# A Mamba-2 block with a ternary FFN on one core: a new order for the last two sequences' steps

## The chip, the cores and the metric

The kernel runs on one core of a Trainium2 chip. The core has five engines that run side by side, each working through its own queue of instructions in order: TensorE (PE in the profile, its weight loads PEld), VectorE (DVE), ScalarE (ACT), GpSimd (POOL) and SyncE (SP, which here only starts DMA transfers). They wait for each other through semaphores. The metric is the device time of one execution in microseconds (us); lower is better. Three runs of the kernel before took 1191.03, 1191.05 and 1191.07 us, with a median of 1191.05 us.

## The reference

The input is x with 16 sequences of 512 tokens and 256 features, in float32. Cut to what matters, each sequence goes through this:

```python
x1 = layernorm(x)
z, xBC, dt = split(x1 @ in_proj_w.T)                 # 512, 768 and 8 columns
xs, B, C = split(silu(causal_conv4(xBC) + conv_b))   # 512, 128, 128
dt = softplus(dt + dt_bias); dA = exp(-dt * exp(A_log))
for t in range(512):                                 # 8 heads of 64
    S = dA[t] * S + (xs[t] * dt[t]) outer B[t]
    y[t] = S @ C[t] + D * xs[t]
g = y * silu(z)
att = x1 + (g * rsqrt(mean(g * g) + 1e-5) * norm_w) @ out_proj_w.T
x2 = x + layernorm(att)
x3 = layernorm(x2)
ffn = gelu(x3 @ ternary(W1).T + b1) @ ternary(W2).T + b2
out = x2 + layernorm(ffn)
```

## The kernel before

The sequences are numbered 0 to 15. One of them has 512 tokens, cut into NC = 4 chunks c of P = 128. The scan over time is done chunk by chunk: inside a chunk as a masked product, and from chunk to chunk through a state of 128x512 values. The work on a sequence b is split into stages, written as generators that issue a few instructions, yield an amount of work, and go on when they are asked again:

- `stage_a*` and `stage_b0`, `stage_d`, `stage_b1` make the projections, the convolution, the step sizes, the decay factors (`dec`), the masked decay matrices (`mts`, one for each chunk) and the tile `ct`, which `stage_d` fills by a DMA of 1.5 MB.
- `stage_e(b)` (L525) multiplies `ct` by C, one POOL instruction on 128x1024 values for each of the chunks 1, 2 and 3.
- `stage_b2(b)` (L555) is the scan. `prepare(c)` transposes the chunk (PE `px`), scales it (DVE `xdt`), makes the products of B and C (PE `pg`), copies B (DVE `bT`), scales the chunk for the state (POOL `xend`) and multiplies into `mts` (DVE, L608). Then, for each chunk, PE computes the chunk's own state (`pst`, L625); POOL decays the old state and DVE adds (`state`, L630 and L633); PE computes the outputs `py` (L641, and from chunk 1 on also L648, which reads the old state and `ct`); DVE adds the skip term (`y`, L654); POOL multiplies by the gate (`zs`, L658). `squares(c, y)` squares on ACT (L569) and adds twice on POOL (L570, L571); `root` sums over features on PE (`pss`, L577) and takes the inverse root on POOL (L582).
- `stage_c1(b)` (L672) begins with the squares of the last chunk, then runs out_proj for the four chunks (PE `po`, L707) with the layer norm statistics of `att` on DVE. After the fourth chunk `second_stream` makes x2 (DVE, L693) and its statistics; `normal` makes x3 (ACT, L285); then x3 is transposed (PE `pt_f`, L733) and split into three bfloat16 parts `x3p` (ACT L736, DVE L737 `rests`, ACT L740, POOL L741).
- `stage_c2(b)` (L745) is the FFN: eight blocks `ph` (PE, L753), each with a gelu (ACT, L759) into `hT`, and then four chunks of `pf` (PE, L787), each followed by DVE (`o`, L793), layer norm, the addition of x2 on POOL (L779) and the DMA of the result. The first two blocks are opened with the first two bfloat16 parts and closed with the third.
- `ending()` (L825) issues the last half of the previous sequence's result: two DVE instructions (L293), one on POOL (L779), one DMA.

The order within each engine's queue is the order in which the program issues the instructions; `manual_schedule` fixes it for PE, ACT, POOL and DVE. What interleaves the stages is `interleave` (L812). A stream is a tuple of stage, its whole work w, a start lo and an end hi. The stream whose position is lowest goes next, and on a tie the one listed first:

```python
at = [lo + (hi - lo) * done / w for _, w, lo, hi, done in live]
i = at.index(min(at))
```

Most of the kernel is a loop in which each sequence's projections stand beside the out_proj of the sequence before, and its scan beside that sequence's FFN. At the end there is nothing left to project. After `stage_a6(15)`, one call of `interleave` (L905) holds the last half of the result of sequence 13, the out_proj and FFN of sequence 14, and `stage_e`, the scan and the out_proj of sequence 15. The call after it runs the FFN of sequence 15 alone.

Tiles live in rings of a fixed number of buffers. PSUM has three: `ps_a` (4 buffers: `px`, `pst`, `py`, and `po` of sequence 15), `ps_tr` (2: `pg`, `pss`, `pt_f`) and `ps_c` (2: `po` of sequence 14, `ph`, `pf`). A new tile waits until the one that had its buffer has been read. In SBUF, `ct`, `att` (shared by `att` and x3), `hT`, `o` (shared with `rests` of sequence 14), `x2` of sequences 0 to 14, `x3p` and `sq` have a single buffer; `y`, `xdt`, `bT`, `xend` and `state` have two.

Of the kernel before, what the change touches and what calls it, by code (L numbers as in the profile page):

```python
# [57 lines left out]
def mamba_ffn_kernel(  # L58
# [18 lines left out]
    NB = x.shape[0]  # L77
# [16 lines left out]
    def load_x(b):  # L94
        xt = io.tile([P, NC, DM], F32, tag="xin", name=f"xin_{b}")
        nc.sync.dma_start(xt, x[b].rearrange("(c p) d -> p c d", p=P))
        xin[b] = xt
# [427 lines left out]
    def stage_e(b):  # L525

        s = seqs[b]
        xbc, ct = s["xbc"], s["ct"]
        for c in range(1, NC):
            nc.gpsimd.tensor_tensor(  # L530
                ct[:, c - 1], ct[:, c - 1],
                xbc[:, 5, c * P : (c + 1) * P].unsqueeze(1).to_broadcast([P, NH, P]), ALU.mult,
            )
            yield 0.7 if c == 1 else 0.15
# [20 lines left out]
    def stage_b2(b):  # L555
        s = seqs[b]
        dt, xbc, zs, dec, mts = s["dt"], s["xbc"], s["zs"], s["dec"], s["mts"]
        ct = s.pop("ct")

        def over_d(t):  # L560
            return t.unsqueeze(2).to_broadcast([P, NH, HD])
# [110 lines left out]
    def stage_c1(b):  # L672
        s = seqs[b]
        g, x1 = s["zs"], s["x1"]
        att = one.tile([P, NC, DM], F32, tag="att", name=f"att_{b}")
        s.pop("squares")()
        rms = s["rms"]

        last = b == NB - 1
        if last:  # L680
            x2 = io.tile([P, NC, DM], F32, tag="xin", name=f"x2_{b}")
            rests = io.tile([P, NC, DM], F32, tag="xin", name=f"rests_{b}")
            rests = rests.rearrange("p c d -> p (c d)").rearrange("p (k t) -> p k t", k=2)
        else:
            x2 = one.tile([P, NC, DM], F32, tag="x2", name=f"x2_{b}")
        x3 = one.tile([P, NC, DM], F32, tag="att", name=f"x3_{b}")
        norm_c, norm_f = Norm(att, f"c{b}"), Norm(x2, f"f{b}")

        def second_stream(lo, hi):


            for c in range(lo, hi):
                nc.vector.scalar_tensor_tensor(  # L693
                    x2[:, c, :], att[:, c, :], norm_c.rs[:, c : c + 1], xin[b][:, c, :],
                    ALU.mult, ALU.add,
                )
                norm_f.stats(c)
            norm_f.offset(lo, hi)

        yield 0.05  # L700
        for c in range(NC):
            if last:
                po = ps_a.tile([P, L], F32, tag="a", name=f"po_{b}_{c}")
            else:
                po = ps_c.tile([P, L], F32, tag="c", name=f"po_{b}_{c}")
            for k in range(NJ):
                nc.tensor.matmul(  # L707
                    po[:, 0:DM], g[:, k, c * P : (c + 1) * P], wo_sb[:, k, :],
                    start=(k == 0), stop=(k == NJ - 1),
                )  # L710
            if c == 2:
                s.pop("root")()
            nc.vector.scalar_tensor_tensor(  # L713
                att[:, c, :], po[:, 0:DM], rms[:, c : c + 1], x1[:, c, :], ALU.mult, ALU.add
            )
            norm_c.stats(c)
            if c % 2 == 1:
                norm_c.shift(c - 1, c + 1)
            if c == 3:
                second_stream(0, 2)  # L720
                second_stream(2, 4)
                if b + 3 < NB:
                    load_x(b + 3)
            yield (0.1, 0.07, 0.01, 0.33)[c]
        norm_f.normal(x3, 0, 1, 2, 3)
        yield 0.22
        if not last:
            rests = one.tile([P, 2, L], F32, tag="o", name=f"rests_{b}")
        x3p = one.tile([P, 3, 2, L], BF16, tag="x3p", name=f"x3p_{b}")
        for k in range(2):  # L730
            pt = ps_tr.tile([P, 512], F32, tag="tr", name=f"pt_f{b}_{k}")
            for c in range(NC):
                nc.tensor.transpose(  # L733
                    pt[:, c * P : (c + 1) * P], x3[:, c, k * P : (k + 1) * P], ident
                )
            nc.scalar.copy(x3p[:, 0, k, :], pt)  # L736
            nc.vector.tensor_sub(rests[:, k, :], pt, x3p[:, 0, k, :])  # L737
        yield 0.12
        for k in range(2):
            nc.scalar.copy(x3p[:, 1, k, :], rests[:, k, :])  # L740
            nc.gpsimd.tensor_sub(x3p[:, 2, k, :], rests[:, k, :], x3p[:, 1, k, :])  # L741
        s.update(x2=x2, x3p=x3p, shift=norm_c.off)
# [69 lines left out]
    def interleave(*streams):  # L812


        live = [[g, w, lo, hi, 0.0] for g, w, lo, hi in streams]
        while live:
            at = [lo + (hi - lo) * done / w for _, w, lo, hi, done in live]
            i = at.index(min(at))
            step = next(live[i][0], None)
            if step is None:  # L820
                live.pop(i)
            else:
                live[i][4] += step

    def ending():  # L825
        while endings:
            endings.pop()()
        yield 0.1
# [4 lines left out]
    E_WORK = 1.0  # L833
    A0_WORK, T0_WORK, A_WORK, A2_WORK, B1_WORK, B2_WORK = 1.0, 0.9, 18.1, 1.0, 0.5, 14.9
    C1_WORK, C2_WORK = 1.0, 24.2
# [10 lines left out]
    def run(stage):  # L846
        for _ in stage:
            pass

    with tc.manual_schedule(engines=ordered):  # L850
        nc.vector.memset(rhs_e[:, 0], 0.0)
        nc.vector.memset(lhs_e, 0.0)
        interleave(
            (
                chain(stage_a0(0), stage_t0(0), stage_a(0, EVEN)),
                A0_WORK + T0_WORK + A_WORK, 0.0, 1.0,
            ),
            (exponent_constants(), 9.0, 0.15, 0.9),
            (stage_a0(1), A0_WORK, 0.4, 0.9),
        )  # L860
        run(stage_t0(1))
        run(stage_a1(0))
        interleave(
            (stage_a2(0), A2_WORK, 0.0, 0.6),
            (scales(), 6.0, 0.35, 0.9),
            (stage_a(1, EVEN), A_WORK, 0.0, 1.0),
        )
        run(stage_a1(1))
        run(stage_b0(0))
        run(stage_d(0))  # L870
        for i in range(NB - 1):
            if i > 0:
                interleave(
                    (ending(), 0.1, 0.0, 0.01),
                    *([(ternary(2), 4.0, 0.1, 0.7)] if i == 1 else []),
                    *([(stage_a6(i), 0.1, 0.02, 0.03)] if i > 1 else []),
                    (stage_a(i + 1, BESIDE), A_WORK - 1.72, 0.0, 1.0),
                    (stage_c1(i - 1), C1_WORK, 0.0, 1.0),
                    (stage_e(i), E_WORK, 0.06, 1.0),
                )  # L880
                run(stage_a1(i + 1))
            second = [
                (stage_b0(i + 1), 0.1, 0.5, 0.51),
                (stage_b1(i + 1, 0, 2), 2 * B1_WORK, 0.68, 0.8),
                (stage_b1(i + 1, 2, 3), B1_WORK, 0.86, 0.9),
                (stage_b1(i + 1, 3, 4), B1_WORK, 0.95, 0.99),
            ]
            if i > 0:
                second.append((stage_c2(i - 1), C2_WORK, 0.02, 1.0))
                second.append((stage_b2(i), B2_WORK, 0.0, 0.98))  # L890
                second.append((stage_a2(i + 1), A2_WORK, 0.15, 0.5))
                second.append((stage_a5(i + 1), 1.7, 0.58, 0.66))
            else:
                second.append((stage_b1(0, 0, NC), 4 * B1_WORK, 0.0, 0.1))
                second.append((stage_e(0), E_WORK, 0.0, 0.3))
                second.append((stage_b2(0), B2_WORK, 0.04, 0.98))
                second.append((stage_a2(1), A2_WORK, 0.03, 0.5))
                second.append((ternary(1), 4.0, 0.3, 0.7))
            second.append((stage_d(i + 1), 0.1, 0.92, 0.93))
            if i + 2 < NB:  # L900
                second.append((stage_a0(i + 2), A0_WORK, 0.6, 0.9))
                second.append((stage_t0(i + 2), T0_WORK, 0.94, 0.97))
            interleave(*second)
        run(stage_a6(NB - 1))
        interleave(  # L905
            (ending(), 0.1, 0.05, 0.06),
            (stage_e(NB - 1), E_WORK, 0.0, 0.25),
            (stage_c1(NB - 2), C1_WORK, 0.0, 0.4),
            (stage_b2(NB - 1), B2_WORK, 0.0, 0.53),
            (stage_c2(NB - 2), C2_WORK, 0.4, 0.98),  # L910
            (stage_c1(NB - 1), C1_WORK, 0.54, 1.0),
        )
        interleave((ending(), 0.1, 0.05, 0.06), (stage_c2(NB - 1), C2_WORK, 0.0, 1.0))

# [42 lines left out]
```

## Time and profile before

| What | Value |
|---|---|
| Median of three runs | 1191.05 us |
| Time of the profiled execution | 1192.11 us |
| Its span, first to last instruction | 1190.4 us |
| PE busy | 1112.2 us (93%), 6104 matmuls |
| DVE busy | 851.5 us (72%) |
| POOL busy | 595.6 us (50%) |
| ACT busy | 564.1 us (47%) |
| Mean granted PE clock | 0.976 of full speed |

The profile is a record of one execution, taken by the hardware profiler. "Busy" is the time in which an engine executed instructions; the rest of the span it waited or had nothing to do. The granted clock is the share of its full speed that PE was allowed. A group of the profile names the line in the kernel, the engine, the operation, and what is written from what; the arrow before a second name tells what ended a wait. All positions below are microseconds from the start of the span.

### The profile page before, as it was taken

The numbers are of one execution on the slowest core, as the hardware profiler recorded it, in microseconds if no ns is written. First come the engines' busy times: TensorE is split into PE (matmuls) and PEld (weight loads), VectorE is DVE, ScalarE is ACT, GpSimd is POOL, SyncE is SP. The second block draws the span as 40 slices with busy tenths as digits, with TensorE's granted clock in tenths as the row PEclk, the third lists the DMA queues.
The fourth block names the chain that finished last, engine by engine and source line by source line (L and its number), as shares of the span: only waits on it lengthen the run. The fifth ranks groups of instructions, "written<-read, shape, count | busy, mean of one in ns | idle before, by whom it ended". The sixth has DMA issues, their size and how long they took to land.

```text
span 1190.4 us, 16908 instructions
## 1 busy us (share of the span) xinstructions
PE 1112.2 (93%) x6104; PEld 731.1 (61%) x6164; DVE 851.5 (72%) x2213; ACT 564.1 (47%) x951; POOL 595.6 (50%) x707
## 2 busy tenths in 40 slices
PE   6746989999999999999999999999999999998697
PEld 2324557575766757576665757566575757666475
DVE  4766786868777686868768686877768687775552
ACT  4531554645454464546356454635546463542321
POOL 2156545545454555546355454635455454545732
PEclk9877999999999999999999999999999999999899
DMA  5010101010110102011020201002020101101000
GB/s 191 2 55 10 65 4 72 18 66 27 36 57 4 71 19 75 19 57 36 4 74 17 73 19 66 27 4 89 4 71 19 66 27 32 44 4 71 2 9 26
DMA packets 28547, 48.57 MB, mean 41 GB/s; under 512 B 6576, under 2 KB 25648, under 8 KB 26416
## 3 DMA queue, kind: packets, MB, share of 16 engines
q1 hardware_dynamic: 27056, 47.33, 11.7%
q8 instruction: 48, 0.79, 0.3%
q10 hardware_dynamic: 1408, 0.16, 0.1%
q14 instruction: 35, 0.29, 0.1%
HBM read 38.44 MB, written 9.04 MB: 40 GB/s over the span
## 4 chain that ended last, share of the span: by engine, by line
PE 83%; POOL 7%; DVE 6%; ACT 3%; issue 1%; DMA 0%; POOLq 0%; ACTq 0%; DVEq 0%
PE pf L787 19%; PE pm L325 14%; PE ph L753 11%; PE po L707 9%; PE pz L347 8%; PE py L641 5%; PE pst L625 4%; PE py L648 3%; POOL x3p L741 3%; PE pe L546 2%; DVE cv L332 2%; POOL xend L605 1%; PE pt_a L303 1%; PE px L590 1%; PE pss L577 1%; PE pt_f L733 1%
## 5 line engine op out<-in xcount | busy, mean ns | idle before, releaser
L332 DVE SCALAR_TENSOR_TENSOR cv<-pm,cw_sb,cv 128x511 f32<-128x511 f32 (+2 forms) x288 | 215.3, 748 | 54.1 <-ACT cv L330 46.2
L787 PE MATMUL pf<-w_sb,hT 128*128 128x256 f32 x1024 | 248.8, 383 | 0.0
L787 PEld LDWEIGHTS pf<-w_sb,hT 128*128 128x128 f32 x1024 | 189.9, 190 | 42.3 <-issue 14.3
L325 PE MATMUL pm<-x1T,win_sb 128*128 128x512 f32 x384 | 187.9, 614 | 5.1 <-ACT x1T L306 5.1
L753 PE MATMUL ph<-x3p,w_bf 128*128 128x512 bf16 x723 | 181.0, 379 | 6.3 <-ACT x3p L740 1.8
L658 POOL TENSOR_TENSOR zs<-y,zs 128x512 f32<-128x512 f32 x64 | 82.4, 1288 | 203.6 <-DVE y L654 203.6
L759 ACT ACTIVATE hT<-ph,b_sb 128x512 f32<-128x512 f32 x128 | 87.9, 688 | 127.9 <-PE ph L753 91.4
L753 PEld LDWEIGHTS <-w_bf 128*128 128x128 bf16 x768 | 72.7, 98 | 93.3 <-issue 28.3
L550 ACT ACTIVATE mt<-pe 128x512 f32<-128x512 f32 x128 | 74.1, 597 | 116.2 <-PE pe L546 114.1
L707 PE MATMUL po<-wo_sb,zs 128*128 128x256 f32 x512 | 124.3, 387 | 0.3 <-DVE att L713 0.3
L330 ACT ACTIVATE cv<-pm,cw_sb 128x512 f32<-128x512 f32 x96 | 65.7, 684 | 123.8 <-PE pm L325 122.2
L347 PE MATMUL pz<-x1T,win_sb 128*128 128x512 f32 x256 | 121.9, 599 | 0.0
L325 PEld LDWEIGHTS pm<-x1T,win_sb 128*128 128x128 f32 x384 | 72.5, 196 | 78.8 <-issue 67.7
L530 POOL TENSOR_TENSOR ct<-ct,xbc 128x1024 f32<-128x1024 f32 x48 | 113.4, 2375 | 12.5 <-DVE sp_a L456 12.5
L707 PEld LDWEIGHTS po<-wo_sb,zs 128*128 128x128 f32 x512 | 95.7, 192 | 28.5 <-issue 17.1
L654 DVE SCALAR_TENSOR_TENSOR y<-xbc,dsk,py 128x128 f32<-128x128 f32 x256 | 71.2, 340 | 44.0 <-PE py L648 23.5
L641 PE MATMUL py<-mt,xdt 128*64 128x128 f32 x1024 | 99.2, 289 | 2.7 <-DVE y L654 2.3
L793 DVE TENSOR_TENSOR o<-pf,b_sb 128x256 f32<-128x256 f32 x64 | 26.9, 420 | 88.1 <-PE pf L787 88.1
L641 PEld LDWEIGHTS py<-mt,xdt 128*64 128x64 f32 x1024 | 62.9, 143 | 32.9 <-issue 18.6
L347 PEld LDWEIGHTS pz<-x1T,win_sb 128*128 128x128 f32 x256 | 47.9, 193 | 56.1 <-issue 48.2
L351 ACT ACTIVATE zs<-pz 128x512 f32<-128x512 f32 x64 | 37.9, 592 | 87.5 <-PE pz L347 87.3
L648 PE MATMUL py<-ct,state 128*64 128x128 f32 x768 | 78.2, 283 | 0.0
(137 smaller groups left out, 1805.3 us busy)
## 6 DMA issues: line engine op xcount, KB each, us to landing
ct<-way SPq DMA_DIRECT2D x16, 1536.0 KB
xin<-in_x SPq DMA_DIRECT2D x16, 512.0 KB
out<-o SPq DMA_DIRECT2D x30, 256.0 KB
w_in<-in_w SPq DMA_DIRECT2D x1, 1024.0 KB
w_sb<-in_w SPq DMA_DIRECT2D x1, 1024.0 KB, 11.0
win_sb<-in_w_in SPq DMA_DIRECT2D x1, 768.0 KB
win_sb<-in_w_in SPq DMA_DIRECT2D x1, 512.0 KB
wo_sb<-in_w_out SPq DMA_DIRECT2D x1, 512.0 KB
```

Source lines behind the costliest of these rows:

```text
L325: nc.tensor.matmul(pm, win_sb[:, k, DI + m * P : DI + (m + 1) * P], x1T[:, k, :], start=(k == 0), stop=(k == 1),)
L332: nc.vector.scalar_tensor_tensor(cv[:, j:], pm[:, 0 : L - j], cw_sb[:, m, 3 - j : 4 - j], cv[:, j:], ALU.mult, ALU.add,)
L347: nc.tensor.matmul(pz, win_sb[:, k, j * P : (j + 1) * P], x1T[:, k, :], start=(k == 0), stop=(k == 1),)
L530: nc.gpsimd.tensor_tensor(ct[:, c - 1], ct[:, c - 1], xbc[:, 5, c * P : (c + 1) * P].unsqueeze(1).to_broadcast([P, NH, P]), ALU.mult,)
L550: nc.scalar.activation(mt[:, hs, :].rearrange("p h t -> p (h t)"), pe, AF.Exp)
L641: nc.tensor.matmul(py[h % 2 * HD : (h % 2 + 1) * HD, j, :], xdt[:, h * HD : (h + 1) * HD], mts[c][:, h, :], start=True, stop=(c == 0),)
L648: nc.tensor.matmul(py[h % 2 * HD : (h % 2 + 1) * HD, j, :], state[:, h * HD : (h + 1) * HD], ct[:, c - 1, h, :], start=False, stop=True,)
L658: nc.gpsimd.tensor_tensor(zs[:, :, tok], y, zs[:, :, tok], ALU.mult)
L707: nc.tensor.matmul(po[:, 0:DM], g[:, k, c * P : (c + 1) * P], wo_sb[:, k, :], start=(k == 0), stop=(k == NJ - 1),)
L753: nc.tensor.matmul(ph, w1_bf[:, k, f * P : (f + 1) * P], x3p[:, j, k, :], start=(j == 0 and k == 0), stop=(j == 2 and k == 1),)
L759: nc.scalar.activation(hT[:, f, :], ph, AF.Gelu, bias=b1_sb[:, f : f + 1])
L787: nc.tensor.matmul(pf[:, 0:DM], hT[:, f, c * P : (c + 1) * P], w2_sb[:, f, :], start=(f == 0), stop=(f == NF - 1),)
```

## The change

Two things are edited. In `stage_b2`, `ct` is read from the sequence's record and no longer removed from it, since `stage_e` now starts after the scan and reads it too. In the call of `interleave` that holds the last steps, the streams' starts, ends and order are changed.

```diff
     def stage_b2(b):
         s = seqs[b]
         dt, xbc, zs, dec, mts = s["dt"], s["xbc"], s["zs"], s["dec"], s["mts"]
-        ct = s.pop("ct")
+        ct = s["ct"]
...
         run(stage_a6(NB - 1))
         interleave(
-            (ending(), 0.1, 0.05, 0.06),
-            (stage_e(NB - 1), E_WORK, 0.0, 0.25),
-            (stage_c1(NB - 2), C1_WORK, 0.0, 0.4),
-            (stage_b2(NB - 1), B2_WORK, 0.0, 0.53),
-            (stage_c2(NB - 2), C2_WORK, 0.4, 0.98),
-            (stage_c1(NB - 1), C1_WORK, 0.54, 1.0),
+            (ending(), 0.1, 0.0, 0.01),
+            (stage_c1(NB - 2), C1_WORK, 0.0, 0.235),
+            (stage_e(NB - 1), E_WORK, 0.03, 0.16),
+            (stage_b2(NB - 1), B2_WORK, -0.02, 0.4),
+            (stage_c2(NB - 2), C2_WORK, 0.235, 0.98),
+            (stage_c1(NB - 1), C1_WORK, 0.42, 0.9),
         )
         interleave((ending(), 0.1, 0.05, 0.06), (stage_c2(NB - 1), C2_WORK, 0.0, 1.0))
```

No instruction is added, removed or changed in shape; only the order of the instructions in the queues differs, from the end of `stage_a6(15)` to the start of the FFN of sequence 15.

## The prediction

> **What bounds the kernel now.** I first read the page's rows of busy tenths and granted clock in 40 slices.
>
> ```profile
> PE   6746989999999999999999999999999999998697
> PEclk9877999999999999999999999999999999999899
> ```
>
> From the fifth slice on PE is full, so the kernel is bound by PE except at both ends. The edit touches the end alone. Next I asked for busy times in stretches cut where the stages change (columns: stretch; its length; busy us and count of PE, PEld, DVE, ACT, POOL; granted clock; DMA share; GB/s).
>
> ```profile
> 1084.00:1110.00 26.00, 18.39 (x123) 14.31 (x122) 18.94 (x54) 6.52 (x10) 16.13 (x22) 0.92 0.06 21
> 1110.00:1133.30 23.30, 17.90 (x110) 11.65 (x112) 7.79 (x19) 7.95 (x12) 15.77 (x15) 0.79 0.00 1
> 1133.30:1184.00 50.70, 50.00 (x235) 37.63 (x234) 21.24 (x68) 12.65 (x21) 18.91 (x34) 1.00 0.05 16
> 1184.00:1190.40 6.40, 0.00 (x0) 0.00 (x0) 1.44 (x5) 0.00 (x0) 1.76 (x5) 0.81 0.12 41
> ```
>
> From 1084 to 1133.3 PE is busy 36.3 of 49.3 us: 13.0 us idle, and part of the rest ran at a lower clock. After 1133.3 only 0.7 us is idle until the last matmul, and the closing 6.4 us are DVE, POOL and the last DMA. So what can be won lies before 1133.3. There I read the chain of waits in order of time (start, us, what).
>
> ```profile
> 1108.76 1.00 POOL xend L605
> 1109.75 0.69 POOL y L570
> ...
> 1110.97 1.00 POOL state L630
> 1111.97 2.31 POOL ct L530
> 1114.29 1.23 POOL zs L658
> 1115.51 2.31 POOL ct L530
> ...
> 1119.04 1.01 POOL state L630
> ...
> 1120.68 0.69 DVE rests L737
> 1121.40 1.23 ACT x3p L740 x2
> ```
>
> POOL's queue carries the end from 1108.8 to 1120; then the split of x3_14 (`rests`, `x3p`), which stands behind the second state in DVE's queue, holds the first `ph`. Only then come `py` of chunk 3 and the FFN.
>
> **The change, part by part.** I wrote out both orders by stepping through the two stream lists, and placed each instruction at the later of its engine's becoming free and its last input, with the trace's durations. Done for the old order, this puts `pf` of sequence 14 at 1144.3, where the trace has 1144.38, and no checkpoint on the way off by over 1.6 us. For the new order:
>
> *1. The scan's `prepare(0)`, the ending and `prepare(1)` go ahead of `ct` 1.* In the old queue POOL's first `ct` (2.36 us) stands ahead of `xend` 0, and PE waits for it (1090.07 to 1092.12). Now `xend` 0 follows the leftover root, ending at 1087.52, and is done near 1088.6, so `pst` 0 runs straight after `po` 0, at 1089.8. That removes 2.0 us of idle PE. The ending's DMA moves up with its two DVE instructions (0.8 us, near 1089.4) and its POOL add (1.27 us, done 1091.5); nothing is ahead of it on SP's queue, as the 1.5 MB load of `ct` was issued at 1077.02. `rests` of sequence 14 overwrites the tile it sends, and comes 20 us later.
>
> *2. out_proj of 14 at once.* DVE now works nearly without a pause from 1087.5: two prepares (2x2.47), the ending (0.82), three chunks of `att` (3x1.13), `y` 0 (1.11), small ones (0.33) and 17 gaps of 0.03 make 11.1, less the first `xdt`, done already: 1097.9. The fourth `att` needs the root from POOL, which stands behind `ct` 1 (to 1096.3), a norm's power and offset (1.0) and `zs` 0 (1.27): 1099.3. Then 0.48+0.65+0.17 and gaps put the second stream at 1100.8 (1102.84 in the trace). Four chunks of x2 with statistics and two offsets take 5.1; POOL's power and offset 1.1; ACT's two pairs overlap but for the last 1.1. x3_14 is ready near 1108.2, where it was 1109.9.
>
> *3. `pt_f` moves ahead of `prepare(3)` and `pst` 2 on PE.* PE is through with `py` 1 at 1100.3, so it stands idle for 7.9 us. Behind it wait `px` 3, `pg` 3 and `pst` 2. What they feed isn't late: `pst` 2 is done by 1115.5 and its addition waits for POOL until 1121.4.
>
> *4. POOL's chain gets longer.* From 1107.1 POOL has without a gap `xend` 2 (1.0), two adds of squares (1.18), state 1 (1.0), `ct` 2 (2.36), `zs` 1 (1.27), `ct` 3 (2.36), the split of x3 (2x1.16), two adds (1.18), state 2 (1.0): 13.7 plus 12 gaps of 0.05 is 14.3, so 1121.3. The split is now ahead of state 2; so, though POOL starts 1.6 us earlier, state 2 ends 1.3 us later than in the trace (1120.04). DVE adds (0.69), and `py` 3 starts at 1122.2, against 1122.97.
>
> *5. The FFN's first blocks go ahead of `py` 3.* `ph` 0 and the first part of `ph` 1 (1.29 + 0.86) run at 1115 to 1120 beside the scan. After `py` 3 remain the rest of `ph` 1 (0.43), `ph` 2 to 4 (3x1.30), a wait of 0.4 for the gelu that stands behind the squares of chunk 2 on ACT, and `pss` (0.38). At full clock `py` 3 takes 1.75: 1122.16 + 1.75 + 0.43 + 3.90 + 0.37 + 0.38 = 1129.0 for `ph` 5. In the trace it is 1133.34. **Sum: 4.3 us off.**
>
> *6. The clock.* Before, `py` 3 took 3.49 us (1123.04 to 1126.53), all at half clock.
>
> ```profile
> 1116.29:1119.71 3.42, 3.42 (x33) 3.13 (x33) 0.00 (x0) 0.95 (x2) 3.34 (x4) 0.50 0.00 0
> 1119.71:1123.12 3.41, 1.74 (x12) 0.59 (x10) 2.92 (x7) 1.22 (x2) 0.38 (x2) 1.00 0.00 0
> 1123.12:1126.53 3.41, 3.41 (x32) 3.08 (x32) 0.00 (x0) 1.91 (x2) 3.41 (x4) 0.50 0.00 0
> ```
>
> A stretch of 3.41 us with PE half busy (1.74) was followed by one at 0.50, and that full one by 1.00. The Trainium skill, "TensorE: Matmul & The Clock Gate" (Part 1 and "Why this matters for your kernels"), says that the clock falls after a whole idle window of some 3.4 us, and warns of gaps over about 3 us. It speaks against part 3: behind the idle 7.9 us the transposes, `pst` 2 and more run at half clock; these have 2 to 3 us of slack before `py` 3, so I charge nothing. For the idle 2.4 to 2.7 us before `py` 3 rule and row differ: by the rule the clock stays up and the gain is 4.3; by the row a window with 1.7 us idle is enough, one window at half clock follows, `ph` 5 comes at 1130.3, and the gain is 3.0. The row decides. Whether the gap falls into one window or is cut by a boundary isn't known; shifting the boundary, some two placements in three halve the clock. I charge 0.9 of 1.3: **3.4 us off**.
>
> *7. From `ph` 5 on* the queues keep their order (`ph` 5, `po` 0, `ph` 6, ... `po` 3, `pf`), except that x3_15, its transposes and split move up by two to four steps of `pf`. x3_15 was ready 8.4 us after `po` 3 of sequence 15 (1152.80 against 1144.38); `pt_f` now stands behind ten steps of 0.865, 8.65 us. It fits by 0.2 us; if not, PE waits a few tenths. In exchange x3p is ready before the last FFN, worth at most 0.1. I take zero, and 0.3 either way.
>
> Against the profiled execution: span 1190.4 - 3.4 = 1187.0, with 1.7 us around it 1188.7. The median of the runs is 1.06 below the profiled time, so 1191.05 - 3.4 = **1187.6 us**.
>
> **Rivals.** *The gain is given back on POOL.* The chain of part 4 has a dozen instructions in a row; each 0.1 us on top moves `py` 3 a microsecond. If it starts 0.9 us later than before and at half clock, 1123.9 + 3.49 + 0.43 + 3.9 + 0.4 = 1132.1: 1.2 off, 1189.9 us. For it: POOL's power takes 0.70 or 0.86 by what stands beside it. Against: the same way of adding hits POOL's checkpoints after 1107 within 0.9 us.
>
> *x3_14 becomes the bound, and it is slower.* Place: `pt_f` at L733, with the rest of the scan behind it on PE, and the split ahead of state 2 on POOL. Its casts are ready 2.8 us before POOL reaches the split; from there every microsecond that x3_14 is late counts in full. It costs the whole gain from 2.8 + 3.4 = 6.2 us late (x3_14 at 1114.4); a DVE queue 10 us late would give 1194.9. For it: a chain of some 40 DVE and POOL instructions leads there, now with the two prepares ahead. Against: the chain's checkpoints agreed within 1.4 us in the old order.
>
> *More is won.* If no window is halved and the tail gains its few tenths, 5 us: about 1186. The bound for everything (13 us idle and the lost clock gone) is out of reach, since POOL alone has 31.9 us of work in these 49.3.
>
> **The numbers.** As worked out, 0.66 (own range 1186.5 to 1188.6, from 4.5 to 2.4 off); given back, 0.15 (1188.6 to 1191.5); slower, 0.11; more, 0.08. A measurement can tell 0.2%, 2.4 us, from no change, that is below 1188.7 or above 1193.4. So faster 0.73, same 0.17, slower 0.10. The range 1185.4 to 1190.6 leaves out the slower case and the ends of the two beside it.
>
> **What would show it.** `pst` 0 without a wait near 1090; PE idle some 8 us ahead of `pt_f` at 1108; POOL unbroken from 1107 to 1121 with the split ahead of state 2; `py` 3 near 1122, at half clock or not; `ph` 5 at 1129 to 1130.5 and everything after it shifted alike. It is wrong if x3_14 comes after 1111, if `py` 3 starts after 1124, or if PE waits at `pt_f` of sequence 15.

## The result and the profile after

| | before | after |
|---|---|---|
| Median (lowest to highest), 8 runs each, us | 1190.88 (1189.96 to 1191.43) | 1186.66 (1185.15 to 1188.49) |
| Profiled execution, us | 1192.11 | 1186.32 |
| Its span, us | 1190.4 | 1184.6 |

The ratio of the times is 0.9968, 95% interval 0.9957 to 0.9979: 3.8 us faster, with 2.5 to 5.1 inside the interval. The two profiled executions differ by more, 5.8 us of span; the one of before lay 1.2 us above its median and the one of after 0.3 below.

The stretches of the changed kernel, cut at the same stages (columns: stretch; its length; busy us and count of PE, PEld, DVE, ACT, POOL; granted clock; DMA share; GB/s):

```profile
1084.00:1110.00 26.00, 18.86 (x127) 14.71 (x125) 20.51 (x55) 7.69 (x12) 18.63 (x25) 0.93 0.06 21
1110.00:1127.37 17.37, 15.13 (x106) 8.58 (x107) 7.20 (x19) 6.88 (x10) 13.26 (x12) 0.81 0.01 1
1127.37:1178.02 50.65, 50.21 (x237) 37.63 (x234) 21.63 (x67) 12.60 (x21) 18.65 (x34) 1.00 0.05 16
1178.02:1184.60 6.58, 0.00 (x0) 0.00 (x0) 1.60 (x5) 0.00 (x0) 1.91 (x5) 0.75 0.12 40
```

`ph` 5 starts at 1127.37, where it started at 1133.34. Up to there PE is idle for 9.4 of 43.4 us, where it was 13.0 of 49.3; what follows is some 0.15 us longer. The waits of PE in that stretch (who waited for whom: total us, times, longest), first of before, then of after:

```profile
PE pst L625 <- POOL xend L605: 6.0, 2, 3.9
PE pt_f L733 <- DVE mt L608: 3.2, 1, 3.2
PE ph L753 <- ACT x3p L740: 1.7, 2, 1.4
```

```profile
PE pt_f L733 <- ACT x L285: 5.0, 3, 3.7
PE pg L596 <- DVE rests L737: 2.3, 1, 2.3
PE pg L596 <- ACT xbc L339: 1.7, 1, 1.7
PE py L648 <- DVE state L633: 0.4, 1, 0.4
```

Both waits for `xend` are gone, and so is the wait of the first `ph` for the split of x3. In their place PE waits for x3 itself, and then for the PSUM buffer that `rests` frees. The chain of waits of the changed kernel (start, us, what) has POOL as forecast, without a gap, and with the split (L741) ahead of the second state's decay:

```profile
1106.16 1.00 POOL xend L605
...
1109.38 2.31 POOL ct L530
1111.69 1.23 POOL zs L658
1112.92 2.31 POOL ct L530
1115.23 2.23 POOL x3p L741 x2
...
1118.67 1.01 POOL state L630
1119.68 0.02 issue
1119.70 0.70 DVE state L633
1120.40 0.04 issue
1120.45 0.44 PE py L648 x4
...
1122.20 1.83 PE ph L753 x8
```

### The profile page after: what moved, and what is told of

It reads as the page before. It is cut to its first block, busy times and chain, and to the rows that moved or that the text cites. A ratio compares the mean times of both kernels' runs of the same rounds, so it can differ in the third digit from the quotient of the medians.

```text
span 1184.6 us, 16968 instructions
## 1 busy us (share of the span) xinstructions
PE 1112.2 (94%) x6164; PEld 728.0 (61%) x6164; DVE 851.7 (72%) x2213; ACT 563.8 (48%) x951; POOL 594.6 (50%) x707
## 4 chain that ended last, share of the span: by engine, by line
PE 82%; POOL 7%; DVE 6%; ACT 3%; DMA 1%; issue 1%; SPq 0%; POOLq 0%; ACTq 0%
PE pf L787 19%; PE pm L325 13%; PE ph L753 12%; PE po L707 9%; PE pz L347 8%; PE py L641 5%; PE pst L625 4%; PE py L648 3%; POOL x3p L741 3%; PE pe L546 2%; DVE cv L332 2%; POOL xend L605 1%; PE px L590 1%; PE pt_f L733 1%; POOL ct L530 1%; PE pt_a L303 1%
## 5 line engine op out<-in xcount | busy, mean ns | idle before, releaser
L787 PEld LDWEIGHTS pf<-w_sb,hT 128*128 128x128 f32 x1024 | 189.9, 190 | 42.3 <-issue 14.3
L753 PE MATMUL ph<-x3p,w_bf 128*128 128x512 bf16 x768 | 189.0, 381 | 2.6 <-ACT hT L759 0.4
L658 POOL TENSOR_TENSOR zs<-y,zs 128x512 f32<-128x512 f32 x64 | 82.3, 1286 | 201.4 <-DVE y L654 201.4
L608 DVE SCALAR_TENSOR_TENSOR mt<-mt,pg 128x1024 f32<-128x1024 f32 x64 | 77.6, 1212 | 0.5
```

Of the source, the lines that this page charges most:

```text
L608: nc.vector.scalar_tensor_tensor(mts[c], mts[c], 1.0, cbt.unsqueeze(1).to_broadcast([P, NH, P]), ALU.min, ALU.mult)
L658: nc.gpsimd.tensor_tensor(zs[:, :, tok], y, zs[:, :, tok], ALU.mult)
L753: nc.tensor.matmul(ph, w1_bf[:, k, f * P : (f + 1) * P], x3p[:, j, k, :], start=(j == 0 and k == 0), stop=(j == 2 and k == 1),)
L787: nc.tensor.matmul(pf[:, 0:DM], hT[:, f, c * P : (c + 1) * P], w2_sb[:, f, :], start=(f == 0), stop=(f == NF - 1),)
```

## The experiments

In all of them the one call of `interleave` is replaced by a written order: each letter takes one step of a stream, `n` the ending, `c` and `d` the out_proj of sequences 14 and 15, `e` the products on `ct`, `b` the scan, `f` the FFN of 14.

```python
def in_order(order, **streams):
    for key in order:
        next(streams[key], None)
```

The old and the new order, in three parts (front, middle, tail), with the same instructions in every queue as the two kernels:

```diff
-"ecbcbnbnccbc" "bbebecebbcbcfbffffbffb" "dfdfdfddffffffffdfffffdffdff"
+"bncbncbecbcc" "bbebceecbcbfbffbfffbfb" "dfdfdfddffffffdffffdffdfffff"
```

The ratios are against runs of the kernel before that were made beside each kernel's own. Where they blur, the profile gives a second measure: the length from the first `px` of these steps to the end of the last instruction, and to the first `pf` of sequence 14. Neither contains anything from before the edit (in these 14 traces the first `px` itself starts anywhere from 1084.56 to 1088.39 us).

| Kernel | Ratio to before (95%) | First `px` to end, us | to first `pf` | Half clock behind `pg` 0 |
|---|---|---|---|---|
| before | 1 | 105.72 | 59.53 | no, later |
| after | 0.9968 (0.9957 to 0.9979) | 99.76 | 53.43 | no |
| e1, new front only | 0.9991 (0.9982 to 1.0) | 103.47 | 57.29 | yes |
| e2, old front, rest new | 0.9978 (0.9968 to 0.9987) | 102.51 | 56.17 | no, later |
| e3, FFN blocks late | 0.9989 (0.9982 to 0.9996) | 102.52 | 56.18 | no |
| e4, scan ahead of transposes | 1.0009 (1.0 to 1.0018) | 105.59 | 59.26 | yes |
| e5, old tail | 0.9970 (0.9958 to 0.9981) | 100.12 | 53.94 | yes |
| e6, PE kept busy in two gaps | 0.9977 (0.9968 to 0.9985) | 101.72 | 55.38 | yes |
| e7, first `ct` early | 0.9965 (0.9952 to 0.9978) | 99.16 | 52.84 | no |
| e8, split late | 0.9963 (0.9950 to 0.9977) | 99.85 | 53.52 | yes |
| e9, PE kept busy in three gaps | 0.9964 (0.9951 to 0.9977) | 100.27 | 53.96 | yes |
| e10, e7 and e8 together | 0.9955 (0.9943 to 0.9967) | 98.74 | 52.41 | no |
| e11, e10 with PE kept busy | 0.9959 (0.9947 to 0.9972) | 100.57 | 54.26 | yes |
| e12, e10 with the old tail | 0.9962 (0.9947 to 0.9976) | 100.25 | 54.08 | yes |

The last column is needed to read the two before it. In every kernel PE waits 1.7 us for its first `pg`, behind the first `px`. The granted clock changes at the borders of windows of 3.41 us (a half clock lasts so long, or a whole multiple, 10.24 us in the changed kernel), and these borders lie elsewhere in each execution. The queues of e10 and e12 are the same up to the first `pf`. Here are the window with most of that gap and the window behind it, in e10 and then in e12:

```profile
1084.81:1088.22 3.41, 2.08 (x15) 1.65 (x13) 1.86 (x6) 2.90 (x4) 1.02 (x3) 1.00 0.22 77
1088.22:1091.63 3.41, 3.08 (x19) 2.87 (x20) 2.40 (x5) 0.80 (x2) 3.41 (x4) 1.00 0.00 0
```

```profile
1084.06:1087.48 3.42, 1.76 (x15) 1.49 (x14) 1.86 (x6) 3.06 (x4) 1.77 (x4) 1.00 0.22 77
1087.48:1090.89 3.41, 3.41 (x14) 3.05 (x13) 3.06 (x7) 0.06 (x1) 3.41 (x4) 0.50 0.00 0
```

In e10 a border cuts the gap. In e12 the gap lies in one window, the next one runs at half clock, and the first `pf` comes 1.7 us later. In the order of the change the same accident costs 0.5 us (e5 against after). So below a kernel is compared with one that has the same entry in this column, or the 0.5 us are named. A "yes" stands for a half clock that begins 2.3 to 2.8 us behind the first `px`, and "later" for one that begins at 7.7 to 7.8, behind PE's wait for the first `xend`, which the old front has.

The theory: the gain is a sum of an earlier front and of FFN blocks that stand ahead of `py` 3, with POOL's chain and the split of x3 deciding when `py` 3 starts. Rivals: the front alone; the clock alone; order of the FFN blocks without effect.

**e1 and e2: the front alone, and everything but the front.**

```diff
-"bncbncbecbcc" "bbebceecbcbfbffbfffbfb" "dfdfdfddffffffdffffdffdfffff"
+"bncbncbecbcc" "bbebecebbcbcfbffffbffb" "dfdfdfddffffffffdfffffdffdff"   # e1
+"ecbcbnbnccbc" "bbebceecbcbfbffbfffbfb" "dfdfdfddffffffdffffdffdfffff"   # e2
```

> Only the first dozen steps (up to the last out_proj chunk of sequence 14) in the new order, all later steps in the old one. If the gain is a sum of parts, the front is worth what a shorter start saves after the later queue has absorbed part of it: 1.5 us off the kernel before, about 1189.3. If removing the wait for the first xend is the whole gain: 4.2 off, about 1186.7. If the front is absorbed by POOL's chain: no change.

> The opposite: first dozen steps in the old order, all later ones in the new. Sum of parts: 2.4 us off the kernel before, about 1188.4, with PE waiting 2 us for the first xend again. Front is everything: 1190.8. Front is worth nothing: 1186.7.

In the profile e1 takes 2.3 us off and e2 3.2, together 5.5 of the 6.0; the 0.5 that is missing is about what the half clock at the beginning of e1 costs (an estimate from e5 and after). In the ratios it is 1.1 and 2.6 of 3.8. The parts add, and neither is everything. In e1 the wait of 2.0 us for the first `xend` is gone and the old waits after it remain. PE's waits in e1:

```profile
PE pst L625 <- POOL xend L605: 3.9, 1, 3.9
PE pt_f L733 <- DVE mt L608: 3.2, 1, 3.2
```

**e3: the first FFN blocks where they were.** The first part of `ph` 0 goes behind `py` 2, the first part of `ph` 1 and the end of `ph` 0 behind `py` 3; everything else is as changed.

```diff
-"bbebceecbcbfbffbfffbfb"
+"bbebceecbcbbfbfffffbfb"
```

> As changed, but the first FFN blocks (first part of ph 0 behind py 2, first part of ph 1 and the end of ph 0 behind py 3) where the old order had them. If having them done ahead of py 3 is a main part: py 3 starts as early as with the change but 2.2 us of PE work more comes after it, so some 2 us of the gain go, about 1189. If the gain comes from POOL's chain and the clock alone: about 1186.7.

The second state is ready as early as with the change (its addition begins 34.91 us behind the first `px`, against 34.89), but 2.8 us are lost in the profile and 2.5 by the ratio. PE's waits in e3 show more than the moved work:

```profile
PE ph L753 <- ACT hT L759: 1.5, 1, 1.5
PE py L648 <- DVE state L633: 1.2, 1, 1.2
```

PE runs dry ahead of `py` 3 (1.2 us, against 0.4 with the change), and again behind it, where `ph` 2 waits for the first gelu (1.5, against nothing). `py` 3 goes on at the same point, 35.7 us behind the first `px`; behind it stand six matmuls of `ph` more (1.3 us) and the wait for the gelu, together the 2.8. The 2.2 us of moved work expected above were too much, since the first part of `ph` 0 still stands ahead of `py` 3. The rival that this order has no effect falls.

**e4: the scan's third chunk ahead of the transposes again.**

```diff
-"bbebceecbcbfbffbfffbfb"
+"bbebceebbccfbffbfffbfb"
```

> As changed, but prepare 3 and pst 2 ahead of the transposes of x3 again. On the sum of parts the split of x3 then comes after state 2 on DVE's queue (the old order's fault), ph 0 waits for it near 1119 with py 2 behind it on PE, and py 3 comes at 1125: no gain is left, about 1190.8. If the idle gap ahead of the transposes only costs time (clock), this is as fast as the change or faster, 1186 or less.

The whole gain is gone. The wait moves back to the split, behind the second state in DVE's queue; the chain of waits of e4:

```profile
1117.03 1.01 POOL state L630
1118.04 0.02 issue
1118.07 0.06 DVE state L633
1118.13 0.55 issue
1118.68 0.69 DVE rests L737
1119.37 0.02 issue
1119.39 0.63 ACT x3p L740
1120.02 0.04 issue
1120.06 0.59 PE ph L753
```

`py` 2 stands behind this `ph` and begins at 1121.24, at half clock; `py` 3 begins at 1126.41, where 1125 was forecast. The first `pf` comes 5.3 us later than in e5, which begins alike. Not all of that is the wait: `py` 2 takes 3.6 us at half clock, against 2.0 with the change. But most of it is, so the gain hangs on the order that lets PE idle ahead of `pt_f`: there the transposes and the split go ahead of work that isn't due. That the gap only costs time, the rival, is refuted.

**e5: the old tail.**

```diff
-"dfdfdfddffffffdffffdffdfffff"
+"dfdfdfddffffffffdfffffdffdff"
```

> As changed, but x3 of sequence 15, its transposes and split at their old places among the pf steps. If the tail is neutral as predicted: the same as the change, within 0.5 us of 1186.7. If the earlier split saves a wait in front of the last FFN: slower by up to 0.3, which the times can't tell; PE's wait at the first ph of sequence 15 in the trace would.

The times agree. In the profile the stretch from the first `pf` to the end is 46.18 us in all four traces with the old tail and 46.31 to 46.34 in all ten with the new. The new tail costs 0.15 us, repeatably, and the traces show where. With the transposes of x3 of sequence 15 ahead of a chunk of `pf` on PE, DVE's `o` of that chunk and POOL's addition of x2 (L779) come later, and the last part of the split (L741) stands behind this addition on POOL: L779 begins 13.24 us behind the first `pf`, against 12.37 with the old tail, and the split ends at 16.73, against 16.17. The matmul of `ph` that reads it starts at 16.78, where it was 16.63.

**e6 and e9: PE kept busy.** 28 matmuls without a reader fill the gap ahead of `pt_f` and the one ahead of `pg` 3; e9 adds 9 more between `ph` 0 and `py` 3.

```diff
+    def warm(times):
+        pw = ps_a.tile([P, L], F32, tag="a", name=f"pw_{times}")
+        for _ in range(times):
+            nc.tensor.matmul(pw, w1_bf[:, 0, 0:P], w1_bf[:, 1, 0:L], start=True, stop=True)
+        yield 0.1
...
-"bbebceecbcbfbffbfffbfb"
+"bbebwceecbcbfbffbfffbfb"    # e6: w is warm(20); prepare(3) holds warm(8)
+"bbebwceecbcbfbffwbfffbfb"   # e9: the second w is warm(9)
```

> As changed, with 28 added matmuls whose result nobody reads: 20 in the idle stretch after py 1 and 8 between px 3 and pg 3, there only to keep PE busy. If the half clock after these two gaps matters: no stretch at 0.50 between 1105 and 1130, times 1 to 1.5 us lower than the change (about 1185.4) and closer together than its 3.3 us from lowest to highest. If the slack ahead of py 3 hides the slow clock: the same median, 1186.7, and the same spread.

> The kernel with 28 added matmuls, and 9 more between the end of ph 0 and py 3, where that kernel's PE stood idle for 2.2 us and then ran py 3 at half clock. If the half clock at py 3 is what made that kernel slower than the change: py 3 at full clock in about 1.8 us, the stretch from the first px of these steps to the end of the span back from 101.7 to 99.8 us, times as with the change (ratio about 0.9965, 1186.7). If the added matmuls cost something else (rings, bandwidth): it stays near 0.9977 and 101.7 us.

e6 fits neither expectation. In the profile it is 1.4 us slower than e5, which has the same half clock at its beginning and the change's order up to the first `pf` (55.38 against 53.94); by the ratios it looks slower too, but the intervals overlap. The stretches of after, of e6 and of e9 around `py` 3 (same columns as above):

```profile
1112.00:1118.00 6.00, 6.00 (x41) 3.39 (x41) 2.35 (x4) 2.86 (x4) 6.00 (x5) 0.62 0.00 0
1118.00:1120.60 2.60, 2.18 (x18) 0.88 (x16) 0.90 (x3) 0.69 (x1) 1.59 (x3) 1.00 0.00 0
1120.60:1124.00 3.40, 3.40 (x36) 2.15 (x35) 1.95 (x8) 1.20 (x2) 1.76 (x2) 1.00 0.00 0
```

```profile
1112.00:1118.00 6.00, 5.48 (x46) 3.25 (x47) 2.60 (x4) 3.10 (x4) 6.00 (x5) 1.00 0.00 0
1118.00:1120.60 2.60, 0.51 (x5) 0.20 (x4) 0.64 (x2) 0.69 (x1) 1.85 (x3) 1.00 0.00 0
1120.60:1124.00 3.40, 3.29 (x30) 2.51 (x31) 1.64 (x8) 0.63 (x1) 1.50 (x2) 0.62 0.02 5
```

```profile
1112.00:1118.00 6.00, 5.25 (x45) 3.25 (x47) 2.92 (x5) 3.11 (x4) 6.00 (x6) 1.00 0.00 0
1118.00:1120.60 2.60, 2.50 (x14) 1.07 (x13) 0.30 (x1) 0.69 (x1) 2.18 (x4) 1.00 0.00 0
1120.60:1124.00 3.40, 3.09 (x37) 2.11 (x35) 2.51 (x9) 0.61 (x2) 1.27 (x1) 1.00 0.02 5
```

In the changed kernel PE works at half clock until 1116.5 and so has work until shortly before state 2 comes. In e6 it is at full clock, done early, and has only 0.51 us of work from 1118.0 to 1120.6, waiting for a state that POOL delivers no earlier (its addition begins 35.40 us behind the first `px`, against 35.39 in e5). That idle stretch brings the half clock down on `py` 3 and the blocks behind it, where nothing hides it. Filling that gap too, e9, brings `py` 3 back to full clock and the time to the level of the change (0.9964). In e9 no gap behind the first halves the clock, in e5 it is at half for 10.2 us, and the first `pf` comes at 53.96 and 53.94. So the slow clock behind these gaps costs nothing, as forecast, and the clock alone isn't the cause of the gain; a late gap at the same place costs what the forecast said it might.

**e7, e8, e10 to e12: a shorter POOL chain.** e7 puts the first `ct` product behind the first `xend` and the ending behind the second out_proj chunk; e8 puts the split behind the second state's decay; e10 does both, e11 adds `warm` of 20, 8 and 9 to e10, e12 the old tail.

```diff
-"bncbncbecbcc" "bbebceecbcbfbffbfffbfb"
+"becbcbcnnbcc" "bbebceecbcbfbffbfffbfb"     # e7
+"bncbncbecbcc" "bbebceecbbcfbffbfffbfb"     # e8
+"becbcbcnnbcc" "bbebceecbbcfbffbfffbfb"     # e10
+"becbcbcnnbcc" "bbebwceecbbcfbfwfbfffbfb"   # e11
```

> As changed, but the first ct product on POOL directly after the first xend, and the ending moved behind the second out_proj chunk. In the trace of the change one DVE instruction on 128x2 values (L260) took 1.50 us instead of 0.17 and ended when the ct product on POOL ended. If DVE is held by the running POOL instruction, it takes 0.17 here, since POOL no longer runs ct then, and the chain to x3 is shorter by up to 1.3 us: about 1185.5 to 1186.5. If the 1.50 us has another cause it stays at 1.5, and the time is the same or up to 0.5 longer.

> As changed, but the split of x3 (two casts on ACT, two subtractions of 1.16 on POOL) behind the second state's decay on POOL. State 2 comes 2.3 us earlier. If PE waits for state 2 in the changed kernel: up to 1.2 us faster, about 1185.5. If PE is the bound there (it is idle 0.4 us ahead of py 3), the gain is at most 0.4, and the end of ph 0 waits for the split: the same, 1186.7, or slower by up to 1.

> Both edits of POOL's order that were tried alone: the first ct product ahead, and the split of x3 behind the second state's decay. POOL's chain to state 2 is then 2.5 to 3 us shorter than with the change. If POOL's chain sets the end: about 1 us faster than the change, 98.7 us from the first px to the end of the span, ratio 0.9955. If PE, at half clock behind its gaps, sets it: 99.5 to 100 us, ratio 0.996 to 0.997.

> The same with 37 added matmuls in PE's three gaps, so that the clock stays at full. If PE at half clock hides the shorter POOL chain: 98.5 us from the first px to the end of the span, ratio 0.9955 or less, the fastest so far. If the split, now last on POOL, holds the end of ph 0 (near 1119.5) whatever the clock: no faster than without the added matmuls, 99.2 or more.

> Both edits of POOL's order as in the fastest kernel so far, with x3 of sequence 15 and its transposes at their old places among the pf steps. If the parts add: 98.74 us from the first px to the end of the span less the 0.17 us that the old places save, so 98.6, and a ratio near 0.9955 again, about 1186.0. If the ratio of 0.9955 was luck: back to 0.997, with 99.8 us.

In e7 L260 takes 0.17 us and the stretch is 0.6 us shorter than with the change. In e8 state 2 comes 2.3 us earlier than in e5 (its addition begins 33.14 us behind the first `px`, against 35.39) and the first `pf` only 0.4: PE, which no longer waits ahead of `py` 3, is the bound there. So with the change POOL's chain holds `py` 3 back by some 0.4 us only, less than the theory had it. e10 is the shortest in the profile, 98.74, 1.0 below the change, though PE now waits for the split:

```profile
PE ph L753 <- POOL x3p L741: 0.9, 2, 0.7
```

e11 and e12 have the half clock at their beginning that e10 lacks, and so the first `pf` at 54.26 and 54.08, against 52.41. Against each other they show that the added matmuls gain nothing, and against e5 (53.94) that the gain of e10 is gone where the clock falls at the beginning. By the times, 0.9955, 0.9959 and 0.9962 overlap with the 0.9968 of the change. None is shown to beat it.

## Why the prediction was right, and where it was off

The forecast was 3.4 us off, 1187.6, in 1185.4 to 1190.6; measured were 1186.66 and, by the ratio, 3.8 off. The mechanism was right: the front, the transposes ahead of the scan, POOL's chain with the split in it, and the FFN blocks ahead of `py` 3. Several sizes were off, and that the sum came out so near is in part luck, as shown below.

- *Part 1, the front:* `pst` 0 starts at 1090.04 without a wait (1089.8 forecast). e1 puts its worth at 2.3 us in the profile, with a half clock in it that the profile of the change doesn't have.
- *Part 2, x3 of sequence 14:* ready at 1107.3, forecast 1108.2. Two errors ran against each other. One norm instruction on DVE (L260) took 1.50 us instead of 0.17, which I didn't see coming; and DVE lost less between instructions than the 0.03 I charged, since neighbours overlap in the record (the second stream took 2.39 us for a pair of chunks, and my sum 2.56).
- *Part 3, the gap ahead of `pt_f`:* PE waits 5.0 us for x3, not 7.9, and 2.3 for `pg` 3. `py` 1 ended at 1101.2, not 1100.3, and I had let the transposes wait for the whole of x3; the first began at 1104.91, with the first chunk. Nothing behind it was late for its user. e4 shows the price of the other order.
- *Part 4, POOL's chain:* this is the term of the sum that was most off. From `xend` 2 to the end of state 2's decay it took 13.55 us (1106.12 to 1119.67) against 14.3; the gaps of 0.05 that I charged weren't there. With the start at 1106.12, not 1107.1, `py` 3 could go on at 1120.45, not 1122.2.
- *Part 5, the FFN blocks:* they stand ahead of `py` 3 as forecast, and e3 prices it at 2.8 us in the profile, 1.3 of moved work and 1.5 for the gelu that `ph` 2 waits for when the blocks come late. The wait of 0.4 for a gelu that I charged didn't come.
- *Part 6, the clock:* I charged 0.9 us for a half clock at `py` 3. In the profiled execution the gap there was 0.42 us, not 2.4 to 2.7, and the clock stayed at 1.00. e6 made the gap 2.2 us long, the clock fell to 0.50, and it lost 1.4. So the row, and not the rule of a whole idle window, was the better guide.
- *Part 7, the tail:* forecast zero, 0.3 either way; it costs 0.15. The transposes fit without a wait, but the split that I expected earlier comes 0.56 us later (e5), since I had left POOL's addition ahead of it out of the sum.

For the profiled pair the sum is the 4.3 of parts 1 to 5 at full clock, 1.7 for the earlier `py` 3 (parts 2 and 4), 0.1 for the later start of the first `px`, less 0.15 in the tail: 6.0, as measured from the first `px` to the end. The forecast of 3.4 was too small for this pair by 2.6, of which 0.9 is the half clock that didn't come.

The runs show some 2 us less than this pair. A part of that is found: the profiled execution of the change had no half clock at the beginning, and six of the eight profiles with its front do; by e5 this costs 0.5 us. Where the rest lies stays open, since the other executions left no profile. The clock's windows lie elsewhere in each of them, and can do more than this: they made 1.7 us of difference between e10 and e12. So a sum that was too small for the profile met runs that gained less than the profile, and that part of the hit is luck.

## What to carry to other kernels

When the last stages of a pipeline drain, look at what each in-order queue holds in front of the chain that ends last, and let an engine that isn't due idle, if this lets the long chain of another engine start earlier. Put work that would follow anyway into the gap ahead of the last dependent step. And before filling idle time to keep a clock up, ask where the engine will stand idle instead: time won ahead of a fixed arrival only moves the gap. When two single profiles are compared, look first whether the clock fell in the same stretches: here the same queues differed by 1.7 us for that reason alone.

## What the runs showed of the hardware

**A DVE instruction can be held until a POOL instruction ends.** The product on POOL and the norm's addition on DVE, in the changed kernel and in e7 (start, us):

```profile
1093.67 2.35 POOL L530 TENSOR_TENSOR ct<-ct,xbc 128x1024 f32<-128x1024 f32 x1
1094.55 1.50 DVE L260 TENSOR_SCALAR rs_c<-mv_c 128x2 f32<-128x2 f32 x1
```

```profile
1090.10 2.36 POOL L530 TENSOR_TENSOR ct<-ct,xbc 128x1024 f32<-128x1024 f32 x1
1095.52 0.17 DVE L260 TENSOR_SCALAR rs_c<-mv_c 128x2 f32<-128x2 f32 x1
```

1093.67 + 2.35 is 1096.02, and 1094.55 + 1.50 is 1096.05. In all eight traces in which the product was running it ended within 0.05 us of it, whatever the point where it began: it took 0.76 in e1, 0.41 in e6. It isn't alone: L453 on DVE (128x32 values, 0.19 us) took 1.26 to 1.28 us 14 times in 48 in the trace of the change, each time with POOL's product L658 running and ending 0.05 us behind it. The Trainium skill, "GPSIMD Engine Reference" (section 1), says that the two engines share their SBUF interfaces and that certain DVE instructions contend. The traces agree; here the price is the rest of the POOL instruction. Not every DVE instruction is held: those on `att` ran beside the same product at their usual 0.43 to 0.48 us.

**The clock falls before a window is wholly idle, and returns late.** Windows of 3.41 us of the changed kernel:

```profile
1106.37:1109.78 3.41, 2.65 (x10) 1.96 (x10) 1.36 (x2) 2.09 (x4) 3.33 (x5) 0.50 0.01 2
1109.78:1113.19 3.41, 1.40 (x4) 1.14 (x5) 3.38 (x10) 1.42 (x3) 3.41 (x3) 0.50 0.01 2
1113.19:1116.61 3.42, 3.42 (x12) 1.08 (x12) 1.20 (x1) 1.67 (x2) 3.42 (x3) 0.52 0.00 0
1116.61:1120.02 3.41, 3.41 (x42) 2.11 (x36) 0.32 (x1) 0.32 (x1) 2.98 (x4) 1.00 0.00 0
```

A window at half clock with PE busy for 2.65 us wasn't enough to bring the clock back; only the full one was (in the kernel before, 2.93 us were enough, from 1109.48 to 1112.90). Before, 1.74 us of work in a window at full clock had not been enough to keep it, and in e12 above 1.76 were not. But 1.79 us in one of the changed kernel (1099.43 to 1102.84) were, so these rows give no sharp limit.
